# Three planned durations in the source-order clock of a two-layer MoE and attention kernel: GpSimd's pause 1.4 to 1.14, attention's norms 8 to 10, attention's tiles 4.6 to 4.9

## The chip, the cores and the metric

The kernel runs on one core of one Trainium2 chip, as one launch in float32. The metric is the device time of one execution in microseconds (us), as the median over several runs. The engines are TensorE (PE, whose weight loads are PEld), VectorE (DVE), ScalarE (ACT), GpSimd (POOL) and SyncE (SP); each runs its own list of instructions in order.

## The reference, cut to what matters

There are 2,048 tokens of 256 numbers in 2 sequences of 1,024. Six residual steps follow each other:

```python
x = x + 0.5 * moe_L0(layernorm(x))          # 8 experts, 2 a token, hidden width 176, and a shared expert of 352
x = x + rwkv(layernorm(x))                  # time mix, then channel mix
x = x + 0.5 * moe_L0(layernorm(x))          # the same weights again
x = x + 0.5 * moe_L1(layernorm(x))          # 32 experts, 6 a token, hidden width 96, and a shared expert of 192
x = x + linear_attention(layernorm(x))      # per sequence: A = sum_s K V / |K|; out = (A * Q) @ Wout
x = x + 0.5 * moe_L1(layernorm(x))
```

A mixture step routes every token to its 2 or 6 best experts and adds the experts' weighted outputs to what the shared expert gives. The linear attention needs the whole of a sequence (1,024 tokens, 8 tiles of 128) before the first of its outputs.

## The kernel before

**Tiling.** Tokens lie in 16 tiles of 128 rows (`x[0]` to `x[15]`); four tiles are a group. The first layer is worked over all 16 tiles, the second by sequence: half A (tiles 0 to 7) and half B (tiles 8 to 15), each with two groups. In the profile's names `L_0A`, `L_0B` are the second layer's first pass over the halves, `L_1A`, `L_1B` its second pass, with attention (`at`) between a half's two passes.

**A mixture step.** For each group, `measure`, `choose` and `plan` norm the rows, score the experts and give each pair of token and expert a slot (`idx`; `soon` is the same for a half's first group, with slots past the first 36 blocks left out). `scatter` (L589) sends the rows to their slots in DRAM (`xs_A`, `xs_B`) by GpSimd's indirect DMAs, 24 for a group of the second layer. `step` then works the slots in blocks of 128 rows, 66 blocks for a half: load (L775), transpose (`px`, L784), gate and up product (`pg`, L806), gating on DVE (`h`, L688), transpose (`ph`, L715), down product (`py`, L824), copy (`yb`, L832), store to `ys_A` or `ys_B` (L834). The first load of a half waits for all of its 48 scatters. `combine` fetches the results back, again by 24 indirect DMAs of GpSimd for a group (`gather`, L846, into 8 buffers `yk`), each followed by an add on DVE (`add_back`, L858). The first group's gathers wait for block 35's store, the second group's for the last block's. After the 66 blocks stands a branch (L979) for further blocks that this data doesn't need; each engine passes it in its own list.

**GpSimd's pauses.** After each third indirect DMA, `pause` puts five small memsets (L330, L333) on GpSimd.

**Attention of a half** (`attend`). For each group: `norms` (DVE statistics, normalization into `axl`, transposes `pt_at`, L156), which waits until the group's gathered rows are added, then `tile_of` for four tiles (two products, L1247, rotation on DVE, L1255 to L1278). After both groups the sum over the sequence (`pA_at`, L1316), the output products (`po_at`, L1086 and L1335), and then norm, scores and plan of the half's second mixture pass.

**What sets the order.** The instructions are written out by Python generators that run beside a planned clock, `Clock`. `run(us)` advances it by a planned time for each block (1.41 for the second layer) and lets each waiting generator go on when its time has come. `spent(us, gap)` has two effects: the piece just written takes `us` of the main line's time, so that the next block is planned that much later, and the generator is called again after `gap`. `called` adds `CALL`, 1.27, to GpSimd's planned time for each indirect DMA, `pause` adds `PAUSE`. The generators `second_pass` (attention and routing), `given_rows` (gathers) and `sends` (scatters) are placed among the blocks in this way. A scheduler of the framework then orders the instructions close to that source order, for each engine. On the chip nothing of the planned clock is left but this order: an engine whose next instruction waits also holds up what stands behind it.

Of the kernel before, what the change touches and what calls it, by code (L numbers as in the profile page):

```python
# [57 lines left out]
def macaron_kernel(ctx: ExitStack, tc: tile.TileContext, a: dict, out: bass.AP):  # L58
# [241 lines left out]
    BLOCK = {"L0": 2.45, "L1": 1.41}  # L300
    SHARED = {"L0": 4.0, "L1": 4.8}
    CALL = 1.27
    PAUSE = 1.4
    still = const.tile([P, 96], F32, name="still")
    pauses = {"on": True}

    class Clock:
# [17 lines left out]
        def pause(self):  # L325
# [9 lines left out]
            self.still = d.ins  # L335
            self.pool += PAUSE

# [38 lines left out]
    clock = Clock()  # L376
# [11 lines left out]
    @contextmanager  # L388
    def behind_blocks():
        with ExitStack() as st:  # L390
            for d in clock.block.values():
                st.enter_context(tc.issue_after(d))
            yield
# [7 lines left out]
    def sparse_moe(layer, w, name, x, xs, ys, moe, given=None, out=None, bufs=2, counts="pt"):  # L401
# [487 lines left out]
        def combine(g, rank=0, lag=4):  # L889
# [3 lines left out]
            def add(n):  # L893
                while len(open_) > n:
                    with behind_blocks():
                        add_back(*open_.pop(0))

            for t in range(BT * g, BT * g + BT):
                for k in range(K):
                    since = clock.now  # L900
                    for due in clock.call(rank):
                        yield due
                        if clock.now - since > 3 * CALL + PAUSE:
                            add(0)
# [307 lines left out]
    def wait(done):  # L1212
        while not done():
            yield clock.now + 1.0

    def attend(s, moe, added, result):
# [9 lines left out]
        def norms(g):  # L1226
            ts = slice(g * BT, (g + 1) * BT)
            lg = [xl[:, t, :] for t in range(TPB)][ts]
            rstd, minus[g] = normalize(xs[ts], lg, BT, f"{name}_{g}")
            for c in range(DC):  # L1230
                nc.scalar.copy(
                    xT[:, c, g * TB : (g + 1) * TB], transposed(lg, c, f"{name}_{g}")
                )

            more = small.tile([P, BT], F32, tag="more", name=f"more_{name}_{g}")
            nc.vector.tensor_scalar(more, rstd, 1.0, None, ALU.add)
            for i, xt in enumerate(xs[ts]):
                nc.vector.scalar_tensor_tensor(
                    xt, xt, more[:, i : i + 1], at["b_out"], ALU.mult, ALU.add
                )  # L1240
# [55 lines left out]
        for g in range(TPB // BT):  # L1296
            yield from wait(lambda: g in added)
            with behind_blocks():
                norms(g)
            yield clock.now + 8.0  # L1300
            for t in range(g * BT, (g + 1) * BT):
                with behind_blocks():
                    tile_of(t)
                yield clock.spent(3.0, 4.6)

        nc.vector.tensor_scalar(ss, ss, 1e-24, None, ALU.max)
        nc.scalar.activation(ss, ss, AF.Sqrt)
# [243 lines left out]
    def second_pass(h):  # L1551

        added, result = set(), {}
        clock.begin(0, given_rows(m1[h], range(2), added, 0.5))

        yield from wait(lambda: h in summed)
        yield from attend(h, moe_pool, added, result)
        m2[h] = half(
            1,
            h,  # L1560
            given=result["given"],
            out=out[HT * h * P : (HT * h + HT) * P, :],
        )
        for g in range(2):
            with behind_blocks():
                for t in range(BT * g, BT * g + BT):
                    result["out_of"](t)
            yield clock.spent(7.0, 8.0)
            yield from onward(m2[h], g, ready2[h])
        with behind_blocks():  # L1570
            m2[h]["owners"]()
            m2[h]["weights"](0)
        yield clock.now
# [117 lines left out]
```

## Time and profile before

| | |
|---|---|
| median of 3 runs | 1363.93 us (1363.43 to 1364.95) |
| the profiled execution | 1358.97 us, its span 1357.1 us |
| instructions in the profile | 22840 |
| PE busy | 1225.2 us, 90% of the span |
| DVE, ACT, POOL busy | 708.1, 602.6, 662.0 us |
| indirect DMAs of GpSimd | 512 |
| memsets of the pauses (L330, L333) | 148 and 592, 28.9 and 106.1 us |
| blocks of L_0A, L_0B, L_1A, L_1B | about 680 to 801, 801 to 990, 1078 to 1202, 1201 to 1305 us |

Times inside the profile count from the span's start. Two instants on different engines can be compared; a busy PE includes stretches at a lower granted clock (the column PEclk). "Idle before" names what ended an engine's idle time, as far as the profile can infer it.

### The profile page before, as it was taken

To read this page: it belongs to the slowest core of one execution; us is meant where nothing else is said; L and a number is where in the kernel's file an instruction comes from. 1 tells how busy PE (TensorE), PEld (TensorE's weight loads), DVE (VectorE), ACT (ScalarE), POOL (GpSimd) and SP (SyncE) were. 2 spreads that over 40 slices of the span, in tenths; PEclk is the share of its full clock that TensorE was granted. 3 is DMA by queue.
4 is the path that set the end of the run, shared out by engine and by line. 5 is a ranking of instruction groups with operands and counts; after the bars stand their busy time and mean duration, and the time that the engine had idled before them with its cause. 6 is when DMAs were issued, how large, how long until landed. Compare 5 with 4: busy or idle time off the path is not lost. (4 is left out here: it accounts for less than half of the span.)

```text
span 1357.1 us, 22840 instructions
## 1 busy us (share of the span) xinstructions
PE 1225.2 (90%) x6036; PEld 951.7 (70%) x6036; DVE 708.1 (52%) x2500; ACT 602.6 (44%) x1637; POOL 662.0 (49%) x1302
## 2 busy tenths in 40 slices
PE   7999999899998799999789988998998799999980
PEld 5767765567676677667579976867765578989860
DVE  5433567644414423555345456775577356456663
ACT  5233575865624133443335545443433255555520
POOL 1620543111113710577777654462767557746655
PEclk9799999999998599989969998987899689999995
DMA  9923534891009223533758875642322247878843
GB/s 284 284 71 105 149 97 134 270 305 51 0 0 235 82 86 104 145 106 105 226 159 262 254 212 156 195 132 89 129 80 78 89 137 237 261 225 259 269 132 102
DMA packets 193669, 213.65 MB, mean 157 GB/s; under 512 B 40668, under 2 KB 176508, under 8 KB 193532
## 3 DMA queue, kind: packets, MB, share of 16 engines
q1 hardware_dynamic: 168956, 144.91, 34.7%
q0 software_dynamic: 24576, 67.14, 16.3%
q8 instruction: 59, 0.97, 0.3%
q14 instruction: 78, 0.64, 0.2%
HBM read 101.99 MB, written 109.97 MB: 156 GB/s over the span
## 5 line engine op out<-in xcount | busy, mean ns | idle before, releaser
L846 POOL DMA_INDIRECT yk_L<-ys_L,idx_L x64 | 62.1, 971 | 175.1 <-DMA ys_L<-yb_L 121.3
L333 POOL MEMSET still<- 128x96 f32 x592 | 106.1, 179 | 34.1
L806 PE MATMUL pg_L_b<-L0gu,xbT_L 128*128 x312 | 107.3, 468 | 1.2 <-ACT xbT_L L788 0.6
L589 POOL DMA_INDIRECT xs_L<-xn_L,idx_L x64 | 61.9, 967 | 74.4 <-DVE s_L L174 28.8
L698 PE MATMUL pg_L<-L0sgu,xTs_L 128*128 128x352 f32 x256 | 93.9, 500 | 2.2 <-DVE h_L L688 1.9
L824 PE MATMUL py_L_b<-L0down,hT_L_b 88*128 x312 | 81.4, 383 | 0.0
L824 PEld LDWEIGHTS py_L_b<-L0down,hT_L_b 88*128 88x128 f32 x312 | 58.9, 192 | 19.1 <-ACT hT_L_b L722 0.3
L688 DVE TENSOR_TENSOR h_L_b<-g_L_b,pg_L_b 128x176 f32<-128x176 f32 x78 | 26.1, 335 | 84.4 <-ACT g_L_b L687 78.8
L806 PEld LDWEIGHTS pg_L_b<-L0gu,xbT_L 128*128 128x128 f32 x312 | 55.0, 194 | 20.5 <-issue 1.2
L698 PEld LDWEIGHTS pg_L<-L0sgu,xTs_L 128*128 128x128 f32 x256 | 48.6, 203 | 24.4 <-issue 3.9
L589 POOL DMA_INDIRECT xs_A<-axl_at,idx_L_1A x48 | 47.2, 983 | 36.5 <-DVE soon_L_1A L577 23.5
L589 POOL DMA_INDIRECT xs_B<-axl_at,idx_L_1B x48 | 46.7, 972 | 33.4 <-DVE soon_L_1B L577 19.4
L806 PE MATMUL pg_L_0B_b<-L1gu,xbT_L_0B 128*128 x264 | 60.1, 355 | 2.3 <-DVEq L979 2.2
L1074 PE MATMUL pkk_cm<-mk_cm,w_WkeyT 128*128 128x512 f32 x128 | 58.7, 594 | 2.2 <-DVE mk_cm L1066 1.3
L806 PE MATMUL pg_L_0A_b<-L1gu,xbT_L_0A 128*128 x264 | 58.5, 347 | 1.8 <-DVE h_L_0A_b L688 1.3
L1086 PE MATMUL pkv_cm<-w_WvalT,sk_cm 128*128 128x256 f32 x256 | 58.6, 379 | 0.1
L1086 PEld LDWEIGHTS pkv_cm<-w_WvalT,sk_cm 128*128 128x128 f32 x256 | 48.3, 190 | 13.7 <-issue 7.2
L806 PE MATMUL pg_L_1A_b<-L1gu,xbT_L_1A 128*128 x264 | 56.7, 339 | 0.0
L806 PE MATMUL pg_L_1B_b<-L1gu,xbT_L_1B 128*128 x264 | 55.0, 331 | 1.6 <-issue 0.8
L589 POOL DMA_INDIRECT xs_A<-xn_L_0A,idx_L_0A x48 | 46.8, 974 | 16.6 <-issue 12.9
L687 ACT ACTIVATE g_L_b<-pg_L_b 128x176 f32<-128x176 f32 x78 | 24.8, 318 | 65.2 <-PE pg_L_b L806 63.5
L589 POOL DMA_INDIRECT xs_B<-xn_L_0B,idx_L_0B x48 | 46.6, 970 | 13.2 <-issue 12.3
(667 smaller groups left out, 3292.8 us busy)
## 6 DMA issues: line engine op xcount, KB each, us to landing
xs_A<-zero SPq DMA_DIRECT2D x1, 10112.0 KB
xs_B<-zero SPq DMA_DIRECT2D x1, 10112.0 KB
xb_L<-xs_L SPq DMA_DIRECT2D x78, 128.0 KB
ys_L<-yb_L SPq DMA_DIRECT2D x78, 128.0 KB
xb_L_0A<-xs_A SPq DMA_DIRECT2D x66, 128.0 KB
ys_A<-yb_L_0A SPq DMA_DIRECT2D x66, 128.0 KB
xb_L_0B<-xs_B SPq DMA_DIRECT2D x66, 128.0 KB
ys_B<-yb_L_0B SPq DMA_DIRECT2D x66, 128.0 KB
```

Source lines behind the costliest of these rows:

```text
L333: d = nc.gpsimd.memset(still, 0.0)
L589: d = nc.gpsimd.indirect_dma_start(out=xs, out_offset=bass.IndirectOffsetOnAxis(ap=idx[:, t, k : k + 1], axis=0), in_=sent[g][t - BT * g], ...
L687: nc.scalar.activation(g, pg[:, 0:width], AF.Silu)
L688: nc.vector.tensor_tensor(dst, g, pg[:, width : 2 * width], ALU.mult)
L698: nc.tensor.matmul(pg, xbT[:, c, i * P : (i + 1) * P], w["sgu"][:, c, u, :, :].rearrange("p z w -> p (z w)"), start=(c == 0), stop=(c == D ...
L806: nc.tensor.matmul(pg, xbT[:, c, :], w["gu"][:, c, bass.ds(e, 1), :, :].rearrange("p e z h -> p (e z h)"), start=(c == 0), stop=(c == DC - 1),
L824: mm = nc.tensor.matmul(py, hT[0:HP, k, :], w["down"][:, bass.ds(e, 1), k, :].rearrange("p e d -> p (e d)"), start=(k == 0), stop=(k == C ...
L846: d = nc.gpsimd.indirect_dma_start(out=yk, out_offset=None, in_=ys[0 : (n + lead) * P, :], in_offset=bass.IndirectOffsetOnAxis(ap=of[:, t, ...
L1074: nc.tensor.matmul(ps, w[:, c, oc * P : (oc + 1) * P], src[:, c, :], start=(c == 0), stop=(c == DC - 1),)
L1086: nc.tensor.matmul(ps, src[:, c, i * P : (i + 1) * P], w[:, c, :], start=(c == 0), stop=(c == n - 1),)
```

## The change

Only numbers of the planned clock change; no instruction's operands, sizes or buffers do. `PAUSE` goes from 1.4 to 1.14. After attention's `norms` the main line is now charged 4.0, where it was charged nothing, and the generator comes back after 10.0, not 8.0. After each attention tile the main line is charged 3.5, not 3.0, and the generator comes back after 4.9, not 4.6.

```diff
     CALL = 1.27
-    PAUSE = 1.4
+    PAUSE = 1.14
@@ attend
             with behind_blocks():
                 norms(g)
-            yield clock.now + 8.0
+            yield clock.spent(4.0, 10.0)
             for t in range(g * BT, (g + 1) * BT):
                 with behind_blocks():
                     tile_of(t)
-                yield clock.spent(3.0, 4.6)
+                yield clock.spent(3.5, 4.9)
```

`PAUSE` is also the third part of the bound `3 * CALL + PAUSE` in `combine`, after which waiting adds are written out at once. The instructions of TensorE, VectorE and SyncE stay the same in number and stand in another order. GpSimd gets three pauses more (15 memsets, L330 and L333), and ScalarE one load of its activation table more (L1307).

## The prediction

> **What bounds the kernel now.** I read the page's head first, then the busy time by stages, then GpSimd's timeline, then PE's and DVE's at the places where GpSimd waits or is waited for.
>
> ```profile
> span 1357.1 us, 22840 instructions
> ...
> PE 1225.2 (90%) x6036; PEld 951.7 (70%) x6036; DVE 708.1 (52%) x2500; ACT 602.6 (44%) x1637; POOL 662.0 (49%) x1302
> ```
>
> PE is the bound on the whole, with 132 us idle. The question is in which stretches the idle time lies. Columns below: window, length, then busy time of PE, PEld, DVE, ACT and POOL, granted clock, DMA share, GB/s.
>
> ```profile
> 801.00:980.00 179.00, 158.48 (x811) 130.66 (x810) 112.19 (x373) 79.97 (x244) 91.49 (x188) 0.88 0.47 143
> 1010.00:1078.00 68.00, 53.75 (x205) 36.25 (x203) 41.88 (x123) 15.20 (x46) 50.82 (x104) 0.87 0.24 78
> 1320.00:1357.10 37.10, 0.00 (x0) 0.00 (x0) 12.77 (x27) 0.00 (x0) 21.98 (x23) 0.55 0.36 103
> ```
>
> Three stretches matter: the 0B blocks with attention of half A (PE idle 20.5 us), the stretch before the 1A blocks (PE idle 14.3), and a tail in which PE does nothing and only GpSimd's last gathers run. GpSimd's own list (start, length, instruction, idle before) shows what the second stretch waits for:
>
> ```profile
> 868.65 0.95 POOL L846 DMA_INDIRECT yk_L_0A<-ys_A,idx_L_0A  x1 [0.31 <-issue]
> ...
> 883.96 1.14 POOL L846 DMA_INDIRECT yk_L_0B<-ys_B,soon_L_0B  x1 [13.22 <-DVE x L1238]
> ...
> 926.01 0.95 POOL L846 DMA_INDIRECT yk_L_0B<-ys_B,soon_L_0B  x1 [0.30 <-DVE x L1335]
> ...
> 951.63 1.01 POOL L589 DMA_INDIRECT xs_A<-axl_at,idx_L_1A  x1 [23.53 <-DVE soon_L_1A L577]
> ...
> 994.48 0.98 POOL L846 DMA_INDIRECT yk_L_0B<-ys_B,idx_L_0B  x1 [4.40 <-SPq L979]
> ...
> 1036.16 1.01 POOL L589 DMA_INDIRECT xs_A<-axl_at,idx_L_1A  x1 [0.16 <-issue]
> ...
> 1073.66 1.08 POOL L589 DMA_INDIRECT xs_A<-axl_at,idx_L_1A  x1 [0.30 <-issue]
> ...
> 1319.05 0.95 POOL L846 DMA_INDIRECT yk_L_1B<-ys_B,idx_L_1B  x1 [0.30 <-issue]
> ```
>
> So GpSimd has 24 early gathers of B (883.96 to 927, 43 us), a pause of 23.5 us until the first group's slots for 1A are there, 24 scatters, then after 0B's last block 24 late gathers (41.7 us) and 24 more scatters (38.6 us to the last one's end, 1.6 us each). The last scatter opens the 1A blocks. PE's and DVE's side:
>
> ```profile
> 880.28 0.39 DVE L832 COPY yb_L_0B<-py_L_0B_b 128x256 f32<-128x256 f32 x1
> ...
> 934.71 1.97 PE L156 MATMUL pt_L_1A<-ident,axl_at 128*128 128x128 f32 x8 [4.02 <-DVE axl_at L147]
> ...
> 960.80 1.26 PE L156 MATMUL pt_L_1A<-ident,axl_at 128*128 128x128 f32 x8 [2.35 <-DVE axl_at L147]
> ...
> 1078.32 1.42 PE L784 MATMUL px_L_1A<-ident,xb_L_1A 128*128 128x128 f32 x4 [6.79 <-DMA xb_L_1A<-xs_A]
> ...
> 1305.25 0.42 DVE L832 COPY yb_L_1B<-py_L_1B_b 128x256 f32<-128x256 f32 x1
> ```
>
> The first is block 35's copy; 3.3 us after its end the early gathers begin. The fourth says that the 1A blocks wait for the scatters, 3.6 us from the last one's end. The fifth is the last block's copy, which ends at 1305.67. By the same 3.3 us its gathers could begin at 1309, but they begin at 1319.05: GpSimd is 10.1 us behind with earlier gathers. That is slack for the blocks.
>
> **What the change moves.** The order of the changed kernel, set against this one's, is almost the same for the first 480 us, and moves by some 2 us of work up to 800. From there: the early gathers' adds of A stand 7 to 8 blocks earlier on DVE, and 24 of A's late gathers, not 18, stand ahead of the branch, so GpSimd is done with A some 9 us sooner (worth nothing by itself: it idles 13.2 us there). On PE, attention's first group stands behind 0B block 4, not 11, its second behind 22, not 35, the sum behind 30, not 44, and the routing of 1A's groups behind 33 and 40, not 48 and 55. Thus attention comes 13 to 15 blocks earlier, and blocks 11 to 54 come later.
>
> *Step 1, block 35.* Adding up along each order what an instruction of its kind adds to PE's time here (medians), block 35's down product comes after 775.0 us of work before and 798.6 after. The work 798.6 is reached at 912 now. But routing's first wait (4.02 us idle before pt_L_1A at 934.71) now lies ahead of it too, and what the clock takes after it. In the 5-us windows from 936 and 941 PE was granted 0.50 and 0.64: 2.5 + 1.8 = 4.3 us lost. So 912 + 4.0 + 4.3 = 920, copy and gate bring the first early gather of B to about 925 (883.96 now). Bounds: 911 with neither loss, 930 if the wait doubles.
>
> [...]
>
> *Step 2, a wait on DVE.* The order puts nine early adds of B ahead of the normalization of 1A's second group. GpSimd's ninth gather has 8 gathers, 2 scatters and 2 or 3 pauses ahead of it: about 20 us at 1.7 a gather, and at most 3.6 to land, so 948. PE is at that group's transposes 13.9 us of work behind block 35, 939 by its own pace. With 2 us for the rest of the normalization, PE stands some 11 us where 2.35 now show at 960.80, and the blocks on DVE behind it stand with it: +9. Bounds: 0 if the adds come when PE is slower anyway, 14 with its clock loss.
>
> *Step 3, 0B's last block.* From those transposes (950) to block 65 are 45.6 us of work, where 24.4 took 29 now (1.19). At 1.1 to 1.19 block 65 ends at 1000 to 1004, and 0B's late gathers begin about 1006 (994.48 now; the price of steps 1 and 2 is partly work that is only exchanged). GpSimd's list up to there, 925 + 43 + 17 scatters at 1.6 = 995, doesn't bind.
>
> *Step 4, the scatters.* Ahead of the branch now stand 17 scatters of 1A's first group, not 24, so that 31 follow the late gathers: 1006 + 41.7 + 31 x 1.6 = 1097, + 3.6 = 1101 for the first 1A block, against 1078.3: +23. Shorter planned pauses are three real pauses more (1.1 us each), not shorter ones.
>
> *Step 5, what fills the wait.* The routing of 1B's first group, 6.9 us of PE's work, now stands ahead of the first 1A block, and no longer among the blocks. So the 1A and 1B blocks are late by 23 - 7 = 16. That this work fits ahead: attention 1's second group can start when the late gathers are added (about 1053), and 32 us of work at 1.33 (25.3 us for 19 now) bring it to 1096, just within 1101. It has no cover left; its waits of some 5 us each would be paid beyond that.
>
> *Step 6, the tail.* The adds of 1A and 1B stand 5 to 8 blocks earlier on DVE, which frees the buffers sooner, so the 10.1 us by which GpSimd is behind at the end can go: 16 - 10.1 = +6. What is late next is the last block itself, then 24 gathers and the final store.
>
> Span 1357.1 + 6 = 1363; the profiled execution 1358.97 becomes 1365. The median shown is 5 us above the profiled one, so the forecast is 1370.
>
> **Rivals.** (a) *Faster:* GpSimd's list runs without the wait of step 2 and block 35 comes by 915. Then 0B ends near its old time, the late gathers begin at 995, 1A's blocks at 1090, late by 12 - 7 = 5 or less, and the tail gives back 10: 1358, 1356 at the least, as GpSimd's 72 remaining gathers and 48 scatters keep it busy until some 8 us before its old end. For it speak the adds that come earlier; against it the 31 scatters. It decides when the blocks are late by less than 7.
> (b) *No change:* late by 8 to 12, all of it eaten by the tail's 10.1 us: 1364. Block 35 at 915 with half of step 2 would do.
> (c) *Much slower:* step 5's cover is short and attention 1's waits (the norm's and the route's 5 us each) come behind the scatters, with a clock loss: late by 24 to 29, 1378 to 1383.
> (d) *It does nothing:* the planned clock is not the chip's. Excluded on order, since attention does move 13 blocks; as a time it is (b).
>
> **Chances.** Forecast (+3 to +11) 0.45, (c) and worse 0.17, (b) 0.16, (a) 0.22. A measurement here can tell 0.2%, 2.7 us. So faster 0.22, same 0.16, slower 0.62. The likeliest case's own range is 1367 to 1375. The range 1357 to 1382 takes in (a) and most of (c).
>
> **What would show it.** In the profile after: the first early gather of B at 920 to 930 behind some 50 us of idle GpSimd; PE idle over 8 us before the second pt_L_1A, ended by DVE; late gathers of B from 1004 to 1009; the first px_L_1A at 1096 to 1106; late gathers of 1B within 4 us of the last block's copy. Wrong if B's early gathers start by 910, if the first 1A block starts before 1088, or if GpSimd's backlog stays at 10 us in the tail, which would make it 1380.

## The result, and the profile after

The changed kernel takes 1381.56 us (1378.33 to 1383.60), the kernel before 1364.44 us. The ratio on record is 1.015, with an interval of 1.0104 to 1.0196, in which the quotient of the two medians, 1.0125, also lies: slower, as forecast, but by 17 us (20 by the ratio) where 6 were forecast. The profiled execution after took 1380.66 us, 21.7 more than the one of before, which with 1358.97 lay 5 us under the median of its kernel.

The page's head of the kernel after:

```profile
span 1378.8 us, 22850 instructions
...
PE 1239.7 (90%) x6036; PEld 960.1 (70%) x6036; DVE 703.3 (51%) x2500; ACT 603.4 (44%) x1638; POOL 664.1 (48%) x1317
```

PE executes the same 6036 instructions and is busy 14.5 us longer with them. The table by stage below shows that this is a lower clock, and that nearly half of it lies where PE's order is still the same. GpSimd's timeline after, the lines that answer to those of before:

```profile
865.80 0.95 POOL L846 DMA_INDIRECT yk_L_0A<-ys_A,idx_L_0A  x1 [1.46 <-DVE x L858]
...
937.99 0.95 POOL L846 DMA_INDIRECT yk_L_0B<-ys_B,soon_L_0B  x1 [70.10 <-DVE count_L_1A L493]
...
978.56 0.95 POOL L846 DMA_INDIRECT yk_L_0B<-ys_B,soon_L_0B  x1 [0.30 <-DVE passed_L_1A L643]
...
1011.44 0.98 POOL L846 DMA_INDIRECT yk_L_0B<-ys_B,idx_L_0B  x1 [5.53 <-SPq L979]
...
1053.25 0.95 POOL L846 DMA_INDIRECT yk_L_0B<-ys_B,idx_L_0B  x1 [0.30 <-DVE x L749]
...
1104.56 0.96 POOL L589 DMA_INDIRECT xs_A<-axl_at,idx_L_1A  x1 [0.30 <-issue]
...
1339.92 0.94 POOL L846 DMA_INDIRECT yk_L_1B<-ys_B,idx_L_1B  x1 [2.11 <-DVE h_L_1B L688]
```

GpSimd idles 70.1 us ahead of B's early gathers, which come 54 us later than before. The last scatter of 1A ends 31 us later. And the late gathers of 1B start 4.3 us after the last block's copy, not 13.4. PE and DVE at the same places:

```profile
925.52 1.12 PE L156 MATMUL pt_L_1A<-ident,axl_at 128*128 128x128 f32 x8 [2.88 <-DVE axl_at L147]
...
956.87 1.97 PE L156 MATMUL pt_L_1A<-ident,axl_at 128*128 128x128 f32 x8 [5.52 <-DVE axl_at L147]
...
1109.13 0.69 PE L784 MATMUL px_L_1A<-ident,xb_L_1A 128*128 128x128 f32 x2 [4.09 <-DMA xb_L_1A<-xs_A]
...
1335.19 0.42 DVE L832 COPY yb_L_1B<-py_L_1B_b 128x256 f32<-128x256 f32 x1
```

All of it looks like the forecast, but late: 13 us at B's early gathers, 5 at its late ones, 8 at the first 1A block. By 0B's first block the whole trace is 11.8 us behind the one of before. Where these come from shows in a table by stage. The page leaves block numbers out; here the down products are counted in the trace, and the stages run from the start of one block's down product to another's. "0A start" is L0's block 35 to 0A's block 22, "0B" 0B's block 0 to 65, "1A" 0B's block 65 to 1A's block 22, "1B" 1A's block 65 to 1B's, "tail" from there to the last instruction of an engine.

| us | to L0's block 35 | 0A start | 0B | 1A | 1B | tail |
|---|---|---|---|---|---|---|
| before | 614.7 | 124.2 | 188.2 | 151.3 | 102.4 | 47.4 |
| after | 621.7 | 129.0 | 193.8 | 160.5 | 105.8 | 39.1 |
| difference | +7.0 | +4.8 | +5.6 | +9.2 | +3.4 | -8.3 |

Two stretches that are left out (rest of 0A's and of 1A's blocks) differ by 0.1 us. In the first column PE's order is the same in both kernels for 560 us. The trace also records the granted clock: in both traces it is 1.00 or 0.50, and the stretches at 0.50 in which PE still has work are 3.4, 6.8, 10.2, 13.7, 17.1 and, once in each trace, 44.4 us long. A run of four matmuls of L806 takes 1.64 us at 0.50 and 0.82 at 1.00 (kernel before, at 1079.59 and 1084.92). With this each stage divides into idle time of PE, half of the time that PE was busy at half clock, and a rest. The rest is the same for a stage in both kernels, within 1 us. Up to PE's last instruction idle time went from 94.6 to 110.3 us, and time busy at half clock from 160.5 to 188.4 us, which is 13.9 us lost. What follows PE's last instruction is 8.4 us shorter: 15.7 + 13.9 - 8.4 + 0.5 (the rest) = 21.7. Of the 13.9 us of clock 8.2 fall into the first column (63.6 and 80.1 us at half clock), 6.6 of them into the 560 us in which PE's order is the same.

### The profile page after: what moved, and what is told of

It reads as the page before. It is cut to its first block, busy times and chain, and to the rows that moved or that the text cites. A ratio compares the mean times of both kernels' runs of the same rounds, so it can differ in the third digit from the quotient of the medians.

```text
span 1378.8 us, 22850 instructions
## 1 busy us (share of the span) xinstructions
PE 1239.7 (90%) x6036; PEld 960.1 (70%) x6036; DVE 703.3 (51%) x2500; ACT 603.4 (44%) x1638; POOL 664.1 (48%) x1317
## 5 line engine op out<-in xcount | busy, mean ns | idle before, releaser
L333 POOL MEMSET still<- 128x96 f32 x604 | 108.0, 179 | 34.6
L806 PE MATMUL pg_L_b<-L0gu,xbT_L 128*128 x312 | 108.5, 471 | 0.9 <-ACT xbT_L L788 0.6
L698 PE MATMUL pg_L<-L0sgu,xTs_L 128*128 128x352 f32 x256 | 100.4, 528 | 2.5 <-DVE h_L L688 2.2
L698 PEld LDWEIGHTS pg_L<-L0sgu,xTs_L 128*128 128x128 f32 x256 | 51.4, 215 | 26.6 <-issue 6.9
L806 PEld LDWEIGHTS pg_L_b<-L0gu,xbT_L 128*128 128x128 f32 x312 | 55.2, 195 | 20.2 <-issue 1.2
L806 PE MATMUL pg_L_0B_b<-L1gu,xbT_L_0B 128*128 x264 | 59.8, 353 | 2.6 <-DVEq L979 2.5
L846 POOL DMA_INDIRECT yk_L_0B<-ys_B,soon_L_0B x24 | 23.0, 958 | 78.3 <-DVE count_L_1A L493 70.1
L806 PE MATMUL pg_L_0A_b<-L1gu,xbT_L_0A 128*128 x264 | 58.3, 346 | 0.7 <-DMA xb_L_0A<-xs_A 0.4
L1086 PEld LDWEIGHTS pkv_cm<-w_WvalT,sk_cm 128*128 128x128 f32 x256 | 48.3, 190 | 13.7 <-issue 7.2
L806 PE MATMUL pg_L_1A_b<-L1gu,xbT_L_1A 128*128 x264 | 56.4, 338 | 0.0
L806 PE MATMUL pg_L_1B_b<-L1gu,xbT_L_1B 128*128 x264 | 55.4, 333 | 0.9 <-ACT hT_L_1B_b L722 0.7
L589 POOL DMA_INDIRECT xs_A<-xn_L_0A,idx_L_0A x48 | 46.5, 969 | 17.5 <-issue 12.8
L589 POOL DMA_INDIRECT xs_A<-axl_at,idx_L_1A x48 | 48.1, 1003 | 13.9 <-issue 12.1
```

The source lines that it names most:

```text
L333: d = nc.gpsimd.memset(still, 0.0)
L589: d = nc.gpsimd.indirect_dma_start(out=xs, out_offset=bass.IndirectOffsetOnAxis(ap=idx[:, t, k : k + 1], axis=0), in_=sent[g][t - BT * g], ...
L698: nc.tensor.matmul(pg, xbT[:, c, i * P : (i + 1) * P], w["sgu"][:, c, u, :, :].rearrange("p z w -> p (z w)"), start=(c == 0), stop=(c == D ...
L806: nc.tensor.matmul(pg, xbT[:, c, :], w["gu"][:, c, bass.ds(e, 1), :, :].rearrange("p e z h -> p (e z h)"), start=(c == 0), stop=(c == DC - 1),
L846: d = nc.gpsimd.indirect_dma_start(out=yk, out_offset=None, in_=ys[0 : (n + lead) * P, :], in_offset=bass.IndirectOffsetOnAxis(ap=of[:, t, ...
L1086: nc.tensor.matmul(ps, src[:, c, i * P : (i + 1) * P], w[:, c, :], start=(c == 0), stop=(c == n - 1),)
```

## The experiments

The jobs ran on several chips, on which the kernel before had medians from 1359 to 1397 us, so times are compared within a job only, as a ratio. Stages are compared over all traces, but they differ from job to job too: the two stretches that the table leaves out took 123.5 us in the first trace of the kernel before and 128.4 in e4, the same kernel. The jobs are e1 to e4, e5 to e8, e9 to e12, e13 to e15, and e16 and e17.

| run | what | ratio to before (interval) | 0A start | 0B | 1A | 1B | tail |
|---|---|---|---|---|---|---|---|
| e1 | the changed kernel again | 1.0151 (1.0105 to 1.0197) | 131.9 | 197.6 | 164.1 | 110.2 | 39.4 |
| e2 | PAUSE 1.14 alone | 1.0111 (1.0068 to 1.0154) | 132.3 | 199.1 | 153.2 | 108.3 | 43.4 |
| e3 | attention's counts alone | 1.0125 (1.0070 to 1.0180) | 119.1 | 203.1 | 164.4 | 105.9 | 45.8 |
| e4 | the kernel before again | single run | 128.2 | 195.1 | 150.1 | 108.3 | 47.5 |
| e5 | before, fillers on PE | 1.0031 (0.9998 to 1.0063) | 125.1 | 193.9 | 153.2 | 108.0 | 47.5 |
| e6 | after, fillers on PE | 1.0132 (1.0068 to 1.0197) | 131.3 | 194.0 | 169.5 | 112.7 | 39.5 |
| e7 | after, PAUSE 1.14 from 0A on only | 1.0074 (1.0043 to 1.0105) | 125.2 | 202.8 | 156.7 | 110.4 | 39.7 |
| e8 | PAUSE 1.14 up to 0A only | single run | 134.9 | 197.2 | 159.5 | 107.1 | 48.7 |
| e9 | counts for half A only | 1.0104 (1.0059 to 1.0149) | 125.5 | 196.2 | 153.4 | 106.5 | 51.0 |
| e10 | counts for half B only | 1.0006 (0.9975 to 1.0037) | 124.5 | 193.5 | 156.1 | 105.0 | 46.1 |
| e11 | before, turn tables later | 1.0056 (1.0023 to 1.0088) | 126.2 | 190.6 | 150.6 | 105.2 | 47.3 |
| e12 | after, turn tables later | 1.0114 (1.0063 to 1.0164) | 132.2 | 195.2 | 165.3 | 109.7 | 39.3 |
| e13 | after, counts for half A only | 1.0164 (1.0127 to 1.0201) | 130.0 | 193.4 | 161.0 | 104.4 | 40.1 |
| e14 | after, counts for half B only | 1.0150 (1.0113 to 1.0187) | 129.2 | 193.8 | 162.9 | 103.5 | 39.1 |
| e15 | both pieces ahead | 0.9997 (0.9969 to 1.0025) | 117.5 | 191.6 | 150.6 | 104.7 | 43.8 |
| e16 | the same again | 0.9971 (0.9943 to 0.9999) | 118.3 | 194.3 | 154.0 | 108.2 | 43.5 |
| e17 | both pieces ahead, attention later | 1.0004 (0.9976 to 1.0032) | 121.4 | 191.1 | 159.3 | 107.2 | 46.2 |

**Which part, and how much is chance (e1 to e4).** My first theory was that the parts cost little alone and that their joint effect, 31 scatters behind the branch, carries the loss.

```diff
 e2:  PAUSE = 1.14, the rest as before
 e3:  yield clock.spent(4.0, 10.0) and clock.spent(3.5, 4.9), PAUSE = 1.4
```

> The changed kernel once more, for a second trace of the same order and for an interval. Open: of the 21.7 us between the two profiled executions, 5.6 are there at 500 us, where PE's order is still the same in both. Theory 'chance': that part differs from execution to execution; L0's second pass begins (first py_L of it) within 2 us of 500.3 here, and the time is 12 to 17 us over the kernel before. Rival 'it is the change': it begins at 505 to 507 again, and the time is 17 to 22 us over.

> PAUSE 1.14, attention's counts as before. In its order the two last pieces of 0A's shared expert stand behind the first block's transposes as in the changed kernel, but 0B's block 35 has 11.5 us of work more ahead of it, not 23.6, all 24 early gathers of B stand ahead of the scatters, and 29 scatters of 1A ahead of the branch. Theory 'scatters': what costs is the joint effect, the early gathers that begin behind routing and the 31 scatters that are left behind the branch; so this one loses only some 5 us at the start of 0A's blocks and gets up to 8 us back from the 5 scatters that need not follow: -4 to +5. Rival 'pause': the shorter pause alone carries it, +12 to +17. Rival 'attention': the counts carry it, this one within 2 us.

> Attention's counts as changed, PAUSE 1.4. Order up to 0B's start as before; block 35 has 4.6 us more work ahead; 24 early gathers, then 28 scatters of 1A ahead of the branch, 20 behind it. Theory 'scatters': the first 1A block some 6 us earlier (4 scatters of 1.6 us fewer after the branch), but 4.5 us of work less ahead of it: -5 to +2. Rival 'attention': the norms and routing that now stand ahead of the blocks have lost their cover, +10 to +17 also here. Rival 'pause': within 2 us.

> The kernel before, for a second trace. Theory 'chance': its span is 3 to 7 us longer than the 1357.1 shown, most of that before 500 us. Rival: its milestones up to 800 us lie within 1 us of the first trace.

Measured: the changed kernel is 21 us slower once more (1.0151 of 1384.8). Each part alone costs nearly as much, 15 and 17 us. The theory falls: e3 has its first 1A block 3.3 us earlier than e4 in the same job and is still slower. The costs don't add, since each part makes an order of its own with other waits in it. As to chance: L0's second pass, which began at 500.3 in the trace of before and at 505.9 in that of after, began at 513.6 in e4 and at 517.7 in e1. To L0's block 35 the seventeen runs took 618.4 to 633.3 us, with old and new orders mixed. So the 7.0 us of the first column say nothing of the change. They stand in the difference of the two profiled executions, but not in the stages behind.

**The half clock (e5, e6).** If a wait costs its idle time and about as much again in half clock (the trace of before has 94.6 us of idle time and 160.5 us at half clock, 80 us of time), then keeping PE busy in the waits should win it back.

```diff
-        pt = bank("pt", f"pt_{name}_{c}")
+        pt = bank("pt", f"pt_{name}_{c}"); [nc.tensor.transpose(pt[:, 0:P], ident, ident) for _ in range(0 if c else FILL.get(name, 0))]
+    FILL = {"at_0_0": 14, "at_0_1": 14, "L1_1A_0": 24, "L1_1A_1": 14, "at_1_1": 20, "L1_1B_1": 14}
 (and 40 into px ahead of 1A's first block)
```

> The order before, with transposes of the identity put on PE ahead of seven of its waits in attention and routing (14, 14, 24, 14, 20 and 14 ahead of the transposes of attention's and the routing's groups, 40 ahead of the first 1A block); their result is overwritten by the real ones. Theory 'clock': what a wait costs is its idle time and then some 7 to 14 us at half the granted clock (70 us between 0B's first block and 1A's block 22); with PE kept busy much of that goes: 8 to 18 us faster than the kernel before, half clock in that stretch 20 to 40 us. Rival 'idle': only the waits count, the fillers change nothing: within 3 us. Rival 'work': the fillers are in the way, 3 to 10 us slower.

> The changed order with the same fillers. Theory 'clock': 10 to 20 us faster than the changed kernel, so from 4 us slower to 8 us faster than the kernel before it in time order, about 0 to +8 beside it. Rival 'idle': as the changed kernel, +14 to +22. Rival 'scatters' (GpSimd's list sets the start of 1A's blocks): gains only what lies before and after that, +8 to +14.

Measured: 1.0031 and 1.0132, nothing won. In 0B's stage of e5 against e4 idle time fell by 3.8 us and half clock by 10.0 us (5.0 us of time), and the rest, with the fillers in it, grew by 7.4. All three terms moved as meant and nearly cancel. The half clock is a real part of a wait's price here, but the fillers paid as much for it.

**The start of 0A's blocks (e7, e8, e11, e12).** PAUSE is switched at 0A's first block.

```diff
-    PAUSE = 1.4
+    PAUSE = [1.4]          # e8: [1.14]
...
+    PAUSE[0] = 1.14        # e8: 1.4
     clock.begin(1, second_pass(0))
```

> The changed counts, but PAUSE is 1.14 only from 0A's blocks on and 1.4 up to there. Order up to 0A's blocks as before; attention 13 to 16 blocks earlier than before, 24 early gathers of B (18, 2 scatters, 6), 25 scatters of 1A ahead of the branch, 23 behind it. Theory 'sum of waits': the 4 to 5 us at the start of 0A's blocks go, the rest of the loss (0B's waits and the waits of 1B's routing ahead of and in 1A's blocks) stays: +9 to +14. Rival 'scatters': with 23 behind the branch as before, +2 or less.

> PAUSE 1.14 up to 0A's blocks, 1.4 from there on, attention's counts as before. For the trace: PE waits some 10.5 us ahead of the first 0A block as in the changed kernel and its block 0 comes some 5 us later against the end of L0's blocks than before; attention only 3 to 5 blocks earlier. Time +4 to +10 if 0A's start is a cost of its own, within 2 if it is chance.

Measured: 1.0074 for e7, 10 us over the kernel before where the full change is 21 over, and 125.2 against 134.9 us at 0A's start. (The single run of e8 was 20 us over the median of the kernel before, more than the 4 to 10 expected; single runs of one kernel lie up to 17 us apart on that chip.) Over all traces this stage is the clearest. Eight with the old order there took 119.1 to 128.2 us (mean 124.8). Eight with PAUSE 1.14 up to 0A took 129.0 to 134.9 us (mean 131.4). The two don't overlap, and on each chip that ran both the new order is the longer one: +6.6 us. Of these 3.7 are idle time of PE, 14.3 to 17.4 us in the new order and 10.1 to 13.1 in the old. The other 3 us are half clock, and there the ranges overlap (24.3 to 31.5 us at half clock against 5.2 to 27.4). What differs is seen on PE. Kernel after, the last pieces of 0A's shared expert (`py_L_0A`), the first block's transposes, 0B's routing and the first block (`py_L_0A_b`):

```profile
676.57 1.89 PE L742 MATMUL py_L_0A<-L1sdown,hT_L_0A 96*128 96x256 f32 x8
688.96 1.12 PE L784 MATMUL px_L_0A<-ident,xb_L_0A 128*128 128x128 f32 x4 [10.50 <-DMA xb_L_0A<-xs_A]
...
706.49 0.79 PE L519 MATMUL rank_L_0B<-ident,count_L_0B 32*128 32x128 f32 x2
...
707.48 2.08 PE L742 MATMUL py_L_0A<-L1sdown,hT_L_0A 96*128 96x256 f32 x4
...
713.20 1.91 PE L742 MATMUL py_L_0A<-L1sdown,hT_L_0A 96*128 96x256 f32 x4
...
717.89 0.64 PE L824 MATMUL py_L_0A_b<-L1down,hT_L_0A_b 96*128 x2
```

and the kernel before:

```profile
678.63 2.04 PE L742 MATMUL py_L_0A<-L1sdown,hT_L_0A 96*128 96x256 f32 x4 [6.68 <-DVE x L749]
...
697.15 1.91 PE L742 MATMUL py_L_0A<-L1sdown,hT_L_0A 96*128 96x256 f32 x4
...
701.35 0.79 PE L519 MATMUL rank_L_0B<-ident,count_L_0B 32*128 32x128 f32 x2
...
704.83 1.06 PE L824 MATMUL py_L_0A_b<-L1down,hT_L_0A_b 96*128 x2
```

Before, pieces 6 and 7 lie ahead of the routing's end (rank, 701.35), and block 0 follows it by 3.5 us. After, both lie behind it (706.49), and block 0 follows by 11.4 us. Counted from L0's block 35 the routing ends alike, at 82 to 87 us in all nineteen traces. So PE waits for the routing in either order, and what it could have done meanwhile comes behind. The windows of 30 us there (PEclk is the third figure from the end, behind POOL's count) show how much the clock differs from trace to trace. They are of the kernel after, 0.61, of the kernel before, 0.74, and of e4 and e3, which have the order of the kernel before at this place, 0.61 and 0.85:

```profile
690.00:720.00 30.00, 26.70 (x115) 21.06 (x115) 15.14 (x75) 11.71 (x26) 23.69 (x50) 0.61 0.39 125
...
690.00:720.00 30.00, 29.38 (x159) 25.09 (x158) 16.62 (x78) 11.90 (x36) 23.66 (x53) 0.74 0.48 156
...
690.00:720.00 30.00, 24.11 (x114) 19.57 (x115) 15.05 (x72) 11.72 (x25) 23.35 (x49) 0.61 0.52 162
...
690.00:720.00 30.00, 24.20 (x147) 19.20 (x148) 18.68 (x91) 14.34 (x36) 23.62 (x49) 0.85 0.56 176
```

One wait was followed by more than one stretch of half clock here: in the kernel after, PE waits 10.5 us ahead of the first transposes, from 678.46 to 688.96, and from 681.1 on, still in the wait, the trace has 13.7, 17.1 and 3.4 us at 0.50, each 3.4 us at 1.00 after the one before.

In the new order the first transposes wait for loads of xs_A that stand on SyncE's queue behind attention's turn tables: kernel after, four tables leave from 683.53 to 684.87, the first loads at 685.60, and the transposes start at 688.96. Two runs moved these away.

```diff
-    load_turns(moe_pool)
...
-    clock.begin(1, second_pass(0))
+    clock.begin(1, second_pass(0)); clock.begin(6, load_turns(moe_pool))
 (load_turns is now a generator that issues one pair of tables each 6 us, behind the blocks)
```

> The order before, with the loads and copies of attention's turn tables (L1206, L1207) put among 0A's blocks, from block 8 to 38, and no longer ahead of them. In the traces the first loads of 0A's blocks stand behind these on SyncE's queue and leave at 679.5, 12 us after the last scatter, and PE waits 6.7 us on a VectorE that waits for such a load. Theory 'turn tables': this wait goes, the first block comes 6 to 9 us earlier, and with its half clock it is worth 6 to 14 us: -6 to -14. Rival: the blocks' loads wait for something else, within 3 us.

> The changed order with the turn tables among 0A's blocks in the same way. Theory 'turn tables': what the changed order lost at 0A's start (129 to 135 us from the end of L0's blocks to 0A's block 22, against 119 to 128 in the old order) was the piece of work that it took out of this wait; without the wait the old and the new order need the same there (within 2 us), and this kernel stays 9 to 13 us behind the one with the old order and the same tables, so 0 to +5 beside the kernel before. Rival: the loss at 0A's start is of the order itself; 16 to 20 us behind the old order with the same tables.

Measured: the first transposes came 62.6 us after L0's block 35 in both, not 66.7 to 68.2 as in the other traces. But the stage took 126.2 and 132.2 us, as without it, and the times were 1.0056 and 1.0114. That wait was hidden: the routing behind it ends no sooner (85.3 and 84.5 us). At 0A's start the rival of e12 holds, the loss is of the order itself: +6.0 between e11 and e12. In time it doesn't: e12 lies 8 us behind e11 by the ratios (13 by the medians), not 16 to 20. And e11 is itself 8 us slower than the kernel before, which neither of its two theories allowed; why stays open.

**Attention by halves (e9, e10, e13, e14).**

```diff
-            yield clock.now + 8.0
+            yield (clock.spent(4.0, 10.0) if s == 0 else clock.now + 8.0)      # e10, e14: s == 1
-                yield clock.spent(3.0, 4.6)
+                yield (clock.spent(3.5, 4.9) if s == 0 else clock.spent(3.0, 4.6))
 (e13 and e14 with PAUSE = 1.14)
```

> Attention's changed counts for half A only, PAUSE 1.4. Order as before up to 0B; second group behind block 30 (35 before), routing behind 41 and 49 (48, 55), 28 scatters of 1A ahead of the branch; attention of half B nearly as before. Theory 'sum of waits': the 8 us that 0B took longer with both halves' counts is here too (PE's waits ahead of the normalized groups and the half clock behind them), part of it given back by the 4 scatters: +2 to +8. Rival 'half B': the loss lies in attention of half B, whose routing lost its blocks; here within 2 us.

> Attention's changed counts for half B only, PAUSE 1.4. Order as before up to 0B's last block; the routing of 1B's groups one block earlier among 1A's blocks. Theory 'sum of waits': one block fewer beside a wait: 0 to +5. Rival 'half B': +10 to +15, in the stretch from 0B's last block to 1A's block 22.

> PAUSE 1.14 and attention's changed counts for half A only. Up to 0B's last block the changed order word for word, 31 scatters behind the branch; in attention of half B the count and rank of 1B's first group stand behind 1A's block 0, its second group's transposes behind block 4, nearly as before (1 and 4). Theory 'scatters': from 0B's last block to 1A's block 22 160 to 166 us, as in the changed kernel, and the time within 4 us of it, +14 to +21. Rival 'routing': 150 to 155 us there, +4 to +9.

> PAUSE 1.14 and attention's changed counts for half B only: 24 early gathers and 29 scatters of 1A ahead of the branch, 19 behind it; count and rank of 1B's first group ahead of 1A's blocks, its second group's transposes behind block 2, as in the changed kernel. Theory 'scatters': from 0B's last block to 1A's block 22 148 to 155 us. Rival 'routing': 160 to 166 us there. In time +12 to +16 by the first, +17 to +22 by the second, as 0B's stretch is also longer than before in this order.

Measured: half A's counts alone cost 14 us, half B's alone nothing that can be told (1.0006). In e9 no stage carries this loss; its tail, 51.0, is the longest of all traces. Its order up to 0B's end is that of e3, and the two took 196.2 and 203.1 us in 0B, so one order varies by 7 us there. With attention earlier and no fillers, ten traces took 193.4 to 203.1 us there (mean 197.2); with attention where it was, four took 188.2 to 195.1 (mean 191.9). The ranges overlap, but on each chip that ran both the earlier attention took longer, by 2 to 8 us. So 0B loses some 5 us; what in it costs this was not separated. The 2 to 8 us that I expected of e9 were too few, and where its 14 come from stays open.

For stage 1A both theories of e13 and e14 predicted a split, and there was none: 161.0 with 31 scatters, 162.9 with 19. PE of e13 ahead of the first 1A block:

```profile
1096.24 3.69 PE L463 MATMUL lg_L_1B<-L1router,axT_at 128*128 128x32 f32 x16 [0.46 <-ACT axT_at L449]
...
1101.98 0.79 PE L508 MATMUL rank_L_1B<-taken_L_1B,before 128*128 128x128 f32 x2 [2.05 <-DVE taken_L_1B L202]
1107.92 1.28 PE L784 MATMUL px_L_1A<-ident,xb_L_1A 128*128 128x128 f32 x4 [4.02 <-DMA xb_L_1A<-xs_A]
```

and of e14:

```profile
1087.17 0.69 PE L784 MATMUL px_L_1A<-ident,xb_L_1A 128*128 128x128 f32 x2 [4.58 <-DMA xb_L_1A<-xs_A]
...
1100.76 3.69 PE L463 MATMUL lg_L_1B<-L1router,axT_at 128*128 128x32 f32 x16 [0.57 <-ACT axT_at L449]
...
1109.16 0.79 PE L508 MATMUL rank_L_1B<-taken_L_1B,before 128*128 128x128 f32 x2
```

In e14 the first transposes come 18 us earlier, counted from 0B's last block, and PE then goes through 1B's routing with little beside it. The first block's down product comes 109.7 us after 0B's last block all the same, where it came after 98.2 and 100.3 in e2 and e9. In e13 the routing's scores and ranks stand ahead of the first transposes, and PE then waits 4.0 us for the scattered rows, so e13 doesn't test late scatters without early routing, as it was meant to. Routing ahead of the blocks is enough for the loss: e14 and e3, with 19 and 20 scatters behind the branch, took 162.9 and 164.4. With neither (e2 and e9: 19 or 20 scatters behind the branch, routing among the blocks) the stage takes 153.2 and 153.4. That late scatters alone are enough is not shown: in each trace without fillers that has 28 or 31 behind the branch, 1B's scores stand ahead of the first 1A block as well. Nor is the price of the routing one number: with it ahead of block 0 too, but 23 and 24 scatters behind the branch, e7 and e10 took 156.7 and 156.1.

**The other way (e15 to e17).** PAUSE 1.6 up to 0A puts both pieces ahead of the first transposes; 1.2 behind it leaves attention where it was (1.4 in e17, where it stands 2 to 4 blocks later).

```diff
-    PAUSE = 1.4
+    PAUSE = [1.6]
...
+    PAUSE[0] = 1.2         # e17: 1.4
     clock.begin(1, second_pass(0))
```

> PAUSE 1.6 up to 0A's blocks, 1.2 from there on, attention's counts as before. The order puts both pieces 6 and 7 of 0A's shared expert ahead of the first block's transposes; attention within a block of where it was (second group behind block 34, sum 44, routing 47 and 55), 24 scatters ahead of the branch. Theory 'pieces': from L0's block 35 to 0A's block 22 3 to 6 us less than the old order's mean of 124.5, block 0 within 82 to 86 us of L0's block 35, and the time 2 to 7 us faster than before. Rival: what holds this stretch is the routing alone, 123 to 126 us, time within 2 us.

> The order with both pieces ahead once more. Theory 'pieces': from L0's block 35 to 0A's block 22 at most 120 us again, rank of 0B's second group at 85 and block 0 at 83 us; the time 2 to 7 us faster than before. Rival 'chance': 123 to 126 us there; the old order itself has shown 119.1 once. Rival 'given back': at most 120 us there and the time within 3 us, the gain lost behind it.

> PAUSE 1.6 up to 0A's blocks, 1.4 from there on: the same start of 0A's blocks, attention 2 to 4 blocks later than before, 20 scatters ahead of the branch and 28 behind it. Theory 'pieces': at most 120 us from L0's block 35 to 0A's block 22. Behind it, by the scatters, the first 1A block comes some 6 us later, by the attention that stands later 0B is as before or 2 us shorter: -4 to +4 in time. Rival 'earlier and later attention both cost': +6 or more.

Measured: 117.5, 118.3 and 121.4 us at 0A's start, 5.7 under the old order's mean. Block 0 came 81.1 to 83.1 us after L0's block 35. PE of e16, both pieces in one run ahead of the routing, and its window there, at 0.91:

```profile
691.81 3.72 PE L742 MATMUL py_L_0A<-L1sdown,hT_L_0A 96*128 96x256 f32 x8
...
708.92 0.60 PE L824 MATMUL py_L_0A_b<-L1down,hT_L_0A_b 96*128 x2
...
711.45 0.48 PE L519 MATMUL rank_L_0B<-ident,count_L_0B 32*128 32x128 f32 x2
```

```profile
690.00:720.00 30.00, 24.36 (x151) 19.31 (x152) 18.91 (x86) 14.83 (x37) 23.63 (x49) 0.91 0.58 182
```

With pieces behind, among and ahead of the wait the stage takes 131.4, 124.8 and 119.1 us on average. That pieces behind the wait cost idle time is shown by eight traces against eight, though `PAUSE` also moves some adds and norms on DVE there, so that no run moved the pieces alone. The gain of the pieces ahead is less sure: their idle time, 10.8 to 12.6 us, is that of the old order, all of the gain is half clock (4.3 to 8.8 us of it), and e3 with the old order has the same, 5.2 us and a stage of 119.1. In time e16 is 4 us faster than the kernel before (0.9971), e15 and e17 the same (0.9997 and 1.0004), where 2 to 7 us had been expected of e15 and e16. So this order is at best a few us better than both kernels, and where the rest of its 6 us goes stays open.

## Why the prediction was wrong in size

The direction and the largest term held; the time lay inside the range, near its upper end, but nearly three times as far off as forecast. By its steps, with means over the traces of the same order:

- *"moves by some 2 us of work up to 800", priced at nothing: the step that failed.* The 2 us of work are right. But they are the work that had filled a wait. 0A's start took 131.4 us, not 124.8: +6.6, of which 3.7 are idle time and the rest half clock. The trace of before shows the 6.68 us wait at this place, and the prediction didn't ask what becomes of the pieces beside it.
- *Step 1.* B's first early gather came at 937.99. Less the 11.8 us by which the trace is late at 0B's start, that is 926, for the 925 forecast.
- *Step 2, +9.* PE waited 5.52 us where 2.35 stood: +3.2. Over-sized.
- *Steps 3 to 5, blocks late by 16.* 0B took 195.0 us (four traces of this order) for 191.9 (four), 1A 163.3 for 150.7 (three each): +3.1 + 12.6 = 15.7. The sum is right by luck, for its two parts are not: 0B was to be 11.5 us longer and 1A 4.5. Late gathers to first transposes took 97.7 us (94.9 forecast, 83.8 before), so step 4 holds. What step 5 had wrong is the routing of 1B, which was to fit into that wait and give 7 us back: ahead of the blocks it costs some 10 us even without late scatters (e14 and e3 against e2 and e9).
- *Step 6, the tail gives back 10.* 39.3 for 47.4: -8.1. The late gathers of 1B follow the last block's copy by 4.3 us, where at most 4 were expected.
- *1B's blocks, not priced:* 108.6 for 105.3, +3.3. The single traces overlap, so this may be chance.

The sum is 6.6 + 15.7 + 3.3 - 8.1 = 17.5, and the median moved by 17.1 (20 by the ratio). Stages of one order vary by several us, so that the sum comes out as near as this is in part chance. Of the rivals, (c) came nearest in time, and in part by its own mechanism: attention 1's routing had too little cover, and 1A took 8 us more than steps 4 and 5 gave it. But 0B took 8 us less than forecast, and 0A's start is in no rival. (a) and (b) needed late blocks by less than 12; it was 26 in the trace. The clock price of 4.3 us for a 4 us gap was of the right size: the trace of before has 10.2 us at half clock there, 5.1 us of time. What was missing was a price for a wait that grows by 4 us.

## What to carry to other kernels

When a planner's order changes, look at every wait that shows in the profile before and ask which work fills it and whether that work still stands ahead of what PE waits for. Two microseconds of work on the wrong side of a wait cost 6.6 here, in a stage whose traces spread by 6 to 9 us for one order. Price a wait at its idle time and the half clock behind it together: of the 6.6 us here 3.7 were idle time and some 3 half clock. And don't expect parts of such a change to add: each part alone made 15 and 17 us of the 21.

## What was not expected of the hardware

The granted clock's half stretches, 3.4 to 44.4 us long in the traces of before and after, cost the kernel before 80 of its 1357 us (160.5 us busy at 0.50). The same order took 614.7 and 627.9 us up to L0's block 35 in two executions of the kernel before, in jobs where its medians were 1364.4 and 1384.8. Of these 13.2 us 5.6 are idle time of PE and 7.3 half clock; the rest is the same, 543.8 and 544.1 us. The blocks themselves keep their pace: from 0A's block 22 to its block 35 ten of 13 blocks took 1.41 or 1.42 us in e4 too, at a granted clock of 1.00, but three took 1.54 to 2.24, 19.9 us in all for 18.4.
